# A graph layer on one core: column offsets 32 to a load, and other shares for ScalarE and VectorE

## The chip, the cores and the metric

The kernel runs on one core of a Trainium2 chip. The metric is device time in microseconds (us) of one execution. A core has five engines that run side by side, each with its own instruction stream in order: TensorE (PE; its weight loads are listed as PEld), VectorE (DVE), ScalarE (ACT), GpSimd (POOL) and SyncE (SP, which only issues DMAs here). An engine's sequencer reads instructions, loads registers and puts work in the engine's queue. It can be ahead of the engine.

## The reference

200,000 edges, sorted by destination, join 12,500 nodes of 128 features. Each node averages the normalised features of its sources, adds its own, and goes through three dense layers:

```python
h = jnp.maximum(_layernorm(x, axis=-1), 0.0)          # x: (12500, 128)
msgs = h[src]                                         # src, dst: (200000,), dst sorted
agg = jax.ops.segment_sum(msgs, dst, num_segments=n)
agg = agg / jnp.maximum(deg, 1.0)[:, None]
h = jax.nn.relu(agg @ Wg + h @ Ws + bg)
h = jnp.tanh(h @ W1 + b1)                             # 128 -> 512
h = jnp.tanh(h @ W2 + b2)                             # 512 -> 512
return x + (h @ W3 + b3)                              # 512 -> 128
```

## The kernel before, in words

**Chunks.** The edges are cut into 1563 chunks of 128. For a chunk PE multiplies the 128 source rows with a one-hot matrix (`oh`, 128 edges by a window of 24 nodes), so that the sum lands in an accumulator of a block of 512 nodes (`agg`) or of the edge between two blocks (`edge`). VectorE makes the one-hots of eight chunks at a time, a group (line 540, `onehot`), two groups ahead in the program, in five buffers used in turn: a group waits until PE has used the one that stood in its buffer.

**Three ways to the rows.** 80 "raw" chunks, ten groups spread over the run, are gathered from the raw input at the start and normalised on VectorE. Most others are gathered from the normalised table in HBM by GpSimd, with one indirect DMA for each chunk (line 451, `gather`), up to 26 chunks ahead of PE (`AHEAD`, the buffers of `rows_in`). The remaining chunks are built without a gather. `tab` holds the table turned, features on partitions and nodes along the row, in the core's memory. A chunk's rows turned are 128 of its columns, picked by offsets that stand in registers:

- ScalarE's lane (`column_copies`, `cols1`): one ACTIVATE makes two columns (line 518; 64 for a chunk).
- VectorE's lane (`column_pairs`, `cols2`): one SCALAR_TENSOR_TENSOR makes two columns (line 500).

PE then turns the chunk (line 444), ScalarE copies it out as `turned` (line 518), and PE uses it like gathered rows. VectorE corrects the one-hot of such a chunk (line 547), since the pairs hold a sum and one of two terms.

**Offsets.** `offsets` (line 461) loads `LOADS` offsets from `places` into registers with one TENSOR_LOAD; the instructions behind it name these registers:

```python
loads, vs = nc.values_load_multi_w_load_instructions(
    places[r : r + 1, q // EVERY, p0 : p0 + LOADS], engines=[kind], ...
```

PE loads its own registers in the same way, with the places of its windows (line 654: up to 16 values, fewer where a raw group lies in the row of 16 chunks).

**Order.** The program is written chunk by chunk, and each engine runs it in that order. `SHARES` says how many chunks go to ScalarE's and VectorE's lanes; they are spread evenly over every fourth chunk from number 80 up to 1480 (ScalarE) and 1540 (VectorE). `load_times` spreads the making of columns over the chunks before use: ScalarE's in steps of four columns, 28 chunks ahead, VectorE's in steps of `LOADS` columns, 36 ahead. The turn stands 14 chunks ahead. The dense layers of a finished block are put between the chunks in small pieces; from chunk 1312 on a planner does it by costs.

Of the kernel before, what the change touches and what calls it, by code (L numbers as in the profile page):

```python
# [45 lines left out]
BEHIND = 2  # L46
EVERY = 4
AT = 3
SHARES = 72, 72
FROM, ENDS = 80, (1480, 1540)  # L50
MARGIN = 28
SUMS_AT, BANK = 1 << 25, 2048
AHEAD_OF_USE = 2
EDGE_BANK = 7
TOGETHER = 4
LOADS = 16

# [21 lines left out]
def windowed(ctx, tc, x, src, dst, Wg, Ws, bg, W1, b1, W2, b2, W3, b3, out, flag):  # L81
# [50 lines left out]
    for c in slots:  # L132
        shares = [n / k * (c < end) for n, k, end in zip(SHARES, within, ENDS)]
        owed = [o + n for o, n in zip(owed, [*shares, 1 - sum(shares)])]
# [323 lines left out]
    def offsets(lane, c, p0):  # L458
        r, q = divmod(c, CPR)
        kind = (mybir.EngineType.Activation, mybir.EngineType.DVE)[lane]  # L460
        loads, vs = nc.values_load_multi_w_load_instructions(  # L461
            places[r : r + 1, q // EVERY, p0 : p0 + LOADS], engines=[kind], min_val=TAB_AT,
            max_val=TAB_AT + (N - 1) * 4,
            skip_runtime_bounds_check_because="src holds rows of x, as the indirect DMAs take it to",
        )
        for ld in loads:
            if lane and last:
                tc.add_manual_dep(
                    ld.ins, last[0].ins.name,
                    mybir.DependencyInfo(mybir.DependencyClass.NoSync, mybir.DependencyReason.DATA), reason="issue_after",  # L470
                )
            tc.keep_in_program_order(ld)
        vs = [v.with_bounds(min_val=TAB_AT, max_val=TAB_AT + (N - 1) * 4, guaranteed_mod_val=0, out_of_modulus=4) for v in vs]
        return enumerate(vs, p0)
# [3 lines left out]
    def two(lane, c, p0):  # L478

        by_pair = columns[c].rearrange("p (t i) -> p i t", t=2)  # L480
        at_v = dict(offsets(lane, c, p0))
        for p in range(p0, p0 + LOADS, 2):
            a, b = (tab[:, bass.ds((at_v[q] - TAB_AT) // 4, 1)] for q in (p, p + 1))
            yield p, by_pair[:, p // 2], a, b

    def column_copies():
        for c in lanes[0]:
            columns[c] = ed.tile([P, P], F32, name="cols1", bufs=4)
            for p0 in range(0, P, LOADS):
                for p, to, a, b in two(0, c, p0):  # L490
# [4 lines left out]
    def column_pairs():  # L495
        for c in lanes[1]:
            columns[c] = ed.tile([P, P], F32, name="cols2", bufs=6)
            for p0 in range(0, P, LOADS):
                for p, to, a, b in two(1, c, p0):
# [387 lines left out]
    def load_times(lane):  # L887
# [4 lines left out]
        use = [max(FROM - 46 + MARGIN, use[0] - step), *use]  # L892
        some = LOADS if lane else TOGETHER
        for i in range(len(lanes[lane])):
# [486 lines left out]
```

## Time and profile before

| | before |
|---|---|
| median of 3 runs | 1805.02 us (1799.81 to 1805.12) |
| profiled execution | 1800.16 us |
| its span, first to last instruction | 1798.4 us |
| PE busy | 1399.2 us, 78% |
| VectorE busy | 1034.4 us, 58% |
| ScalarE busy | 1534.3 us, 85% |
| GpSimd busy | 1348.5 us, 75% |
| granted TensorE clock, mean | 0.83 of full speed |

The times are medians of whole executions; the profile is one execution. Busy time counts an engine's own work only: loads of registers and waits are not in it, so an engine that is 58% busy can still have little time to spare. "Issue" in a profile's row is idle time in which the engine waited for no other engine that the profile shows; ahead of the columns it is the load of the offsets.

### The profile page before, as it was taken

The numbers are of one execution on the slowest core, as the hardware profiler recorded it, in microseconds if no ns is written. First come the engines' busy times: TensorE is split into PE (matmuls) and PEld (weight loads), VectorE is DVE, ScalarE is ACT, GpSimd is POOL, SyncE is SP. The second block draws the span as 40 slices with busy tenths as digits, with TensorE's granted clock in tenths as the row PEclk, the third lists the DMA queues.
The fourth block names the chain that finished last, engine by engine and source line by source line (L and its number), as shares of the span: only waits on it lengthen the run. The fifth ranks groups of instructions, "written<-read, shape, count | busy, mean of one in ns | idle before, by whom it ended". The sixth has DMA issues, their size and how long they took to land.

```text
span 1798.4 us, 26668 instructions
## 1 busy us (share of the span) xinstructions
PE 1399.2 (78%) x5410; PEld 926.5 (52%) x5410; DVE 1034.4 (58%) x5580; ACT 1534.3 (85%) x5169; POOL 1348.5 (75%) x1428
## 2 busy tenths in 40 slices
PE   0047576878787888897888888787888888779998
PEld 0036454555455555555555555545555554555567
DVE  7965866666655656566565665556556655435400
ACT  1213999999999999999999999999999999998223
POOL 7777777777777777777777777777777777777774
PEclk9999999767887786877867868879787788778998
DMA  8954222222222222222222222222222222222221
GB/s 209 242 140 139 55 67 58 64 61 70 58 73 71 59 73 71 57 73 71 71 59 71 71 59 71 71 59 73 71 59 71 71 56 73 71 65 71 59 62 45
DMA packets 129832, 138.77 MB, mean 77 GB/s; under 512 B 30119, under 2 KB 106019, under 8 KB 129464
## 3 DMA queue, kind: packets, MB, share of 16 engines
q0 software_dynamic: 45408, 93.09, 19.9%
q1 hardware_dynamic: 80974, 40.37, 8.3%
q10 hardware_dynamic: 3276, 3.51, 0.7%
q14 instruction: 128, 1.05, 0.2%
q8 instruction: 46, 0.75, 0.2%
HBM read 123.84 MB, written 13.03 MB: 76 GB/s over the span
## 4 chain that ended last, share of the span: by engine, by line
ACT 29%; PE 25%; DMA 19%; issue 13%; POOL 9%; ACTq 4%; DVE 0%; DVEq 0%; POOLq 0%
ACT cols L518 25%; DMA rows<-htab,scol 19%; PE pm L441 17%; PE agg L441 6%; POOL rows L451 4%; POOL raw L217 4%; ACTq L461 4%; ACT h L518 3%; PE edge L441 2%; PE pm L444 1%; ACT turned L518 0%; ACT rd L521 0%; ACT o L521 0%; DVE cols L500 0%; DMA raw<-in_x_dram,rsrc 0%
## 5 line engine op out<-in xcount | busy, mean ns | idle before, releaser
L451 POOL DMA_INDIRECT rows<-htab,scol x1339 | 1267.8, 947 | 408.0 <-issue 226.7
L518 ACT ACTIVATE cols<-both_first,tab 128x2 f32<-128x2 f32 x4608 | 1351.2, 470 | 3.8 <-issue 1.9
L441 PE MATMUL pm<-h,w 128*128 128x512 f32 (+4 forms) x1344 | 795.0, 692 | 25.0 <-ACT h L518 20.5
L500 DVE SCALAR_TENSOR_TENSOR cols<-first_only,tab 128x2 f32<-128x2 f32 x4608 | 666.6, 218 | 250.4 <-issue 249.3
L441 PEld LDWEIGHTS agg<-oh,rows 128*128 128x128 f32 x1928 | 394.6, 253 | 426.8 <-DMA rows<-htab,scol 260.5
L441 PE MATMUL agg<-oh,rows 128*128 128x24 f32 x1928 | 398.7, 307 | 177.2 <-DMA rows<-htab,scol 172.2
L540 DVE TENSOR_TENSOR oh<-shared,dloc 128x192 f32<-128x192 f32 x186 | 65.5, 354 | 356.6 <-PE agg L441 211.0
L441 PEld LDWEIGHTS pm<-h,w 128*128 128x128 f32 x1344 | 243.6, 229 | 33.5 <-ACT h L518 22.4
L441 PEld LDWEIGHTS edge<-oh,rows 128*128 128x128 f32 x750 | 144.0, 233 | 164.8 <-DMA rows<-htab,scol 89.4
L441 PE MATMUL edge<-oh,rows 128*128 128x24 f32 x750 | 145.9, 289 | 63.3 <-DMA rows<-htab,scol 59.4
L518 ACT ACTIVATE h<-pm,b2c 128x512 f32<-128x512 f32 (+4 forms) x112 | 76.9, 689 | 51.6 <-PE pm L441 51.6
L217 POOL DMA_INDIRECT raw<-in_x_dram,rsrc x80 | 79.8, 998 | 25.6 <-issue 23.8
L587 DVE TENSOR_SCALAR_CACHE_REDUCE nearby<-nearby,parity 128x656 uint8<-128x656 uint8 x98 | 86.8, 886 | 0.0
L518 ACT ACTIVATE h<-pm,b1c 128x512 f32<-128x512 f32 (+4 forms) x112 | 76.6, 694 | 11.8 <-PE pm L441 11.2
L521 ACT COPY tab<-pm 128x512 f32<-128x512 f32 (+1 forms) x25 | 14.4, 577 | 68.1 <-PE pm L444 68.1
L340 PE MATMUL pm<-ident,idx_f 98*128 98x98 f32 x32 | 5.7, 373 | 82.5 <-DVE idx_f L334 54.4
L441 PEld LDWEIGHTS agg<-oh,turned 128*128 128x128 f32 x196 | 45.1, 258 | 36.6 <-issue 33.0
L444 PE MATMUL pm<-ident,cols 128*128 128x128 f32 x144 | 49.2, 342 | 10.7 <-ACT h L518 5.4
L518 ACT ACTIVATE turned<-pm 128x128 f32<-128x128 f32 x144 | 50.3, 349 | 7.4 <-PE pm L444 7.4
L740 DVE TENSOR_TENSOR mT<-agg,sums 128x136 f32<-128x136 f32 (+6 forms) x57 | 15.3, 272 | 71.3 <-PE agg L441 61.9
L441 PE MATMUL pm<-ident,h 128*128 128x128 f32 (+1 forms) x196 | 43.8, 309 | 14.4 <-ACT h L518 14.3
L270 ACT ACTIVATE sq<-xt 128x1280 f32<-128x1280 f32 (+3 forms) x11 | 12.7, 1153 | 44.6 <-DVE xt L267 35.4
(129 smaller groups left out, 850.8 us busy)
## 6 DMA issues: line engine op xcount, KB each, us to landing
rows<-htab,scol POOLq DMA_INDIRECT x1339
nearby<-bytes_at SPq DMA_DIRECT2D x98, 82.0 KB
xb<-htab SPq DMA_DIRECT2D x24, 256.0 KB
xb<-in_x_dram SPq DMA_DIRECT2D x23, 256.0 KB
out_dram<-o SPq DMA_DIRECT2D x23, 256.0 KB
xt<-in_x_dram SPq DMA_DIRECT2D x8, 640.0 KB
htab<-h SPq DMA_DIRECT2D x8, 640.0 KB
raw<-in_x_dram,rsrc POOLq DMA_INDIRECT x80
```

The costliest lines, as they stand in the source:

```text
L217: nc.gpsimd.indirect_dma_start(out=t[:, j, :], out_offset=None, in_=x, in_offset=bass.IndirectOffsetOnAxis(ap=rsrc[:, g, j : j + 1], axis=0),)
L270: nc.scalar.activation(sq, xt, AF.Square)
L441: tc.keep_in_program_order(nc.tensor.matmul(*a, **k))
L444: tc.keep_in_program_order(nc.tensor.transpose(*a, **k))
L451: nc.gpsimd.indirect_dma_start(out=r, out_offset=None, in_=htab, in_offset=bass.IndirectOffsetOnAxis(ap=scol[:, c : c + 1], axis=0),)
L461: loads, vs = nc.values_load_multi_w_load_instructions(places[r : r + 1, q // EVERY, p0 : p0 + LOADS], engines=[kind], min_val=TAB_AT, max ...
L500: last[:] = [tc.keep_in_program_order(nc.vector.scalar_tensor_tensor(to, first_only, a, b.to_broadcast([P, 2]), op0=ALU.mult, op1=ALU.subtract
L518: tc.keep_in_program_order(nc.scalar.activation(*a, **k))
L521: tc.keep_in_program_order(nc.scalar.copy(*a))
L540: newest[:] = [nc.vector.tensor_tensor(oh[:, :k, :w], lane[:, None, :w].to_broadcast([P, k, w]), dloc[:, g * GRP : g * GRP + k][:, :, None ...
L587: done = nc.vector.tensor_scalar(w, w, parity[:, t % 2 : t % 2 + 1], None, op0=ALU.is_equal, op1=ALU.add, accum_out=found[:, t : t + 1])
L740: nc.vector.tensor_tensor(out, s, t, op=ALU.add)
```

## The change

```diff
-SHARES = 72, 72
+SHARES = 70, 98
-LOADS = 16
+LOADS = 32
```

The first line takes two chunks from ScalarE's lane and gives 26 more to VectorE's. So 168 chunks are built from columns in place of 144, and 1315 are gathered in place of 1339. The chunks of both lanes move to other places, since they are spread anew. The second line makes each load of offsets twice as long: four loads for a chunk in place of eight, each ahead of 16 instructions in place of 8, on both engines. VectorE's steps grow with it from 16 to 32 columns.

GpSimd's queue at the place where the raw gathers end and the others begin, and on to the end of the program (`raw` and `rows` are the buffers written):

```order
 L217 DMA raw_173<-in_x_dram,rsrc 128x128 x8
 L217 DMA raw_182<-in_x_dram,rsrc 128x128 x8
-L451 DMA rows<-htab,scol 128x128 x1339
+L451 DMA rows<-htab,scol 128x128 x1315
 L1346 TENSOR_LOAD flag
```

Nothing else moved there: 24 gathers fewer in one unbroken row.

VectorE's stream where its first columns stand, before (`raw_146` is the sixth raw group, `ohr` a scratch buffer, `oh_204` the first one-hot buffer, in its third use):

```order
L267 SCALAR_TENSOR_TENSOR raw_146<-shared,raw_146 128x1024
L272 TENSOR_TENSOR ohr<-raw_146 128x8x128
L273 TENSOR_REDUCE shared<-ohr 128x8
L540 TENSOR_TENSOR oh_204<-shared,dloc 128x192
L587 TENSOR_SCALAR nearby,found<-nearby,parity 128x656
L547 SCALAR_TENSOR_TENSOR oh_204<-shared,partner,oh_204 128x24
L461 TENSOR_LOAD places
L500 SCALAR_TENSOR_TENSOR cols_1370<-first_only,tab 128x2 x8
```

The same place in the changed kernel:

```order
L267 SCALAR_TENSOR_TENSOR raw_146<-shared,raw_146 128x1024
L461 TENSOR_LOAD places
L500 SCALAR_TENSOR_TENSOR cols_1323<-first_only,tab 128x2 x16
...
L500 SCALAR_TENSOR_TENSOR cols_1648<-first_only,tab 128x2 x16
L272 TENSOR_TENSOR ohr<-raw_146 128x8x128
L273 TENSOR_REDUCE shared<-ohr 128x8
L461 TENSOR_LOAD places
L500 SCALAR_TENSOR_TENSOR cols_1648<-first_only,tab 128x2 x16
L461 TENSOR_LOAD places
L500 SCALAR_TENSOR_TENSOR cols_1648<-first_only,tab 128x2 x16
L540 TENSOR_TENSOR oh_204<-shared,dloc 128x192
```

Seven loads and 112 pairs now stand ahead of the one-hots of that group; before they came behind it.

ScalarE's stream in the middle of the run, before (`cols_22034` is one chunk's columns, `h_512` a dense layer's output):

```order
L461 TENSOR_LOAD places
L518 ACTIVATE cols_22034<-both_first,tab 128x2 x8
L461 TENSOR_LOAD places
L518 ACTIVATE cols_22034<-both_first,tab 128x2 x6
L518 ACTIVATE turned<-pm 128x128
L518 ACTIVATE cols_22034<-both_first,tab 128x2 x2
L461 TENSOR_LOAD places
```

And in the changed kernel:

```order
L461 TENSOR_LOAD places
L518 ACTIVATE cols_27273<-both_first,tab 128x2 x16
L461 TENSOR_LOAD places
L518 ACTIVATE cols_27273<-both_first,tab 128x2 x4
L518 ACTIVATE h_512_27519<-pm,bgc 128x512
L518 ACTIVATE cols_27273<-both_first,tab 128x2 x12
L461 TENSOR_LOAD places
```

The loads stand half as densely; the other work lies between the columns as before.

## The prediction

> **What bounds the kernel now.** I read the page's groups first, to see which engine's work is serial, then the waits, then the windows. These are three groups of the page and the waits of POOL and, from 200 to 1600 us, of PE:
>
> ```profile
> L451 POOL DMA_INDIRECT rows<-htab,scol x1339 | 1267.8, 947 | 408.0 <-issue 226.7
> L518 ACT ACTIVATE cols<-both_first,tab 128x2 f32<-128x2 f32 x4608 | 1351.2, 470 | 3.8 <-issue 1.9
> L500 DVE SCALAR_TENSOR_TENSOR cols<-first_only,tab 128x2 f32<-128x2 f32 x4608 | 666.6, 218 | 250.4 <-issue 249.3
> ...
> POOL rows L451 <- issue: 226.7, 744, 0.3
> POOL rows L451 <- DMA rows<-htab,scol: 75.2, 247, 0.3
> POOL rows L451 <- PE agg L441: 57.6, 189, 0.3
> ...
> PE agg L441 <- DMA rows<-htab,scol: 142.4, 201, 2.2
> PE edge L441 <- DMA rows<-htab,scol: 47.8, 73, 1.6
> PE pm L441 <- ACT h L518: 20.4, 9, 5.6
> ```
>
> GpSimd issues one gather after another. Each costs (1267.8 + 408.0) / 1339 = 1.2515 us with the gap ahead of it, and no wait is longer than 0.3 us, whatever it is put down to: a fixed pace, never held up by a full buffer. In the body PE waits 190 us for gathered rows and 20 us for ScalarE. The last gather of the timeline starts 16.6 us before the end of the 1798.4 us span:
>
> ```profile
> 1781.76 0.94 POOL L451 DMA_INDIRECT rows<-htab,scol  x1 [0.30 <-issue]
> ```
>
> So GpSimd's pace sets the end, and a short tail follows it. ScalarE is nearly as full (3.8 us idle ahead of all its columns) but starts its last load of offsets at 1650.4 us (row below). What comes off the gathers comes off the end only as long as the other engines keep up.
>
> **Fewer gathers.** The change takes 168 chunks off GpSimd, not 144: 1315 gathers, not 1339. 24 x 1.2515 = **30.0 us less**, on the path. Raw gathers, tail and setup stay.
>
> **ScalarE.** A chunk of columns costs it 64 x 1351.2 / 4608 = 18.8 us. Two fewer: -37.5 us. Every chunk off GpSimd is also copied out once after PE turned it, 24 copies more; a group by shape, and two rows of the timeline:
>
> ```profile
> L518 ACT ACTIVATE turned<-pm 128x128 f32<-128x128 f32 x144 | 50.3, 349 | 7.4 <-PE pm L444 7.4
> ...
> 714.59 0.33 ACT L518 ACTIVATE turned<-pm 128x128 f32<-128x128 f32 x1
> 714.75 1.57 ACT L518 ACTIVATE cols<-both_first,tab 128x2 f32<-128x2 f32 x5
> ```
>
> By the mean that is +8.4 us, by the distance to the next start (0.16 us) +3.8. ScalarE saves 29 to 34 us where GpSimd saves 30, so it stays just as close behind. PE gains 24 turns of 0.34 us (8 us, beside its 190 us of waits for rows).
>
> **The longer load.** No trace shows a load of 32 values. The nearest rows are the loads of 16 on the two engines, and PE's loads of window places, which hold 16 values or, where a raw group opens the row, 8 (the loads at 418.9 and 412.3 us):
>
> ```profile
> L461 DVEq TENSOR_LOAD <-places x576: 1093/1123/1781, 172.5 to 1704.4; - x192
> L461 ACTq TENSOR_LOAD <-places x576: 1004/1043/1620, 172.6 to 1650.4; - x192
> ...
> L654 PEldq TENSOR_LOAD <-spots x1: 604/604/604, 412.3 to 412.3; - x1
> ...
> L654 PEldq TENSOR_LOAD <-spots x1: 1137/1137/1137, 418.9 to 418.9; - x1
> ```
>
> Eight more values cost 533 ns, so sixteen more cost 1.07 us: about 2.17 us on VectorE and 2.11 on ScalarE. From below, a load might stay at 1.1 us; from above I let it be 10% over the line, 2.4 us. I take the line: it goes through both of PE's points and 1.04 to 1.12 us of the other engines agree with it at 16. Halving the number of loads then saves next to nothing.
>
> The Trainium skill, "DMA: Bandwidth & Descriptors", section "Latency and other measured facts", gives a register load a floor of about 600 ns, to be spread over more work; with such a fixed part the 392 loads that VectorE is spared for 98 chunks would be worth 235 us of its time, and rival 1 below would be out. PE's load of 8 values at 604 ns is near that figure, but its 1137 at 16 leaves a fixed part of only 71 ns, and the rows decide.
>
> On ScalarE the load is hidden. The columns begin with an unbroken run; the fifth load of that stretch is at 179.7 us:
>
> ```profile
> 173.97 27.13 ACT L518 ACTIVATE cols<-both_first,tab 128x2 f32<-128x2 f32 x97 [1.03 <-DVE oh L547]
> ...
> L461 ACTq TENSOR_LOAD <-places x5: 1020/1027/1218, 172.6 to 179.7; - x5
> ```
>
> Its own first instruction is the 33rd of the run, at 173.97 + 32 x 0.28 = 182.9 us: 3.2 us, or 11 instructions, are queued when the load starts. A load of 2.1 us leaves 1.1 us to spare. Cost: nothing.
>
> On VectorE it isn't hidden, since eight pairs last only 1.1 us:
>
> ```profile
> 701.54 1.14 DVE L500 SCALAR_TENSOR_TENSOR cols<-first_only,tab 128x2 f32<-128x2 f32 x8 [0.97 <-issue]
> 702.99 1.14 DVE L500 SCALAR_TENSOR_TENSOR cols<-first_only,tab 128x2 f32<-128x2 f32 x8 [0.31 <-issue]
> 704.44 1.17 DVE L500 SCALAR_TENSOR_TENSOR cols<-first_only,tab 128x2 f32<-128x2 f32 x8 [0.30 <-issue]
> ```
>
> Sixteen columns take 1.45 us: 1.10 of load and 0.35 in which the sequencer passes on eight pairs. For 32 columns I reckon 2.17 + 0.70 = 2.87 us, while sixteen pairs keep the engine 1.14 + 8 x 0.131 = 2.19 us: 0.68 us idle for each load. That needs about ten pairs queued when the next load starts. VectorE can hold that many:
>
> ```profile
> 724.04 3.33 DVE L500 SCALAR_TENSOR_TENSOR cols<-first_only,tab 128x2 f32<-128x2 f32 x24
> ...
> L461 DVEq TENSOR_LOAD <-places x4: 1097/1107/1116, 719.3 to 724.7; - x4
> ```
>
> The last of these loads, at 724.7 us, belongs to the 17th pair, which starts at 726.1: eleven were ahead of it.
>
> **VectorE's budget from 200 to 1600 us.** All instructions, then the columns' alone (after the length stand the busy us of PE, PEld, DVE, ACT and, in the first, POOL), and VectorE's waits there:
>
> ```profile
> 200.00:1600.00 1400.00, 1153.34 (x4252) 740.23 (x4251) 833.07 (x4921) 1378.98 (x4744) 1058.75 (x1121) 0.80 0.25 66
> ...
> 200.00:1600.00 1400.00, 45.40 (x133) 29.46 (x133) 609.18 (x4215) 1275.95 (x4347) 0.80 0.25 66
> ...
> DVE cols L500 <- issue: 226.1, 486, 1.9
> DVE oh L540 <- PE agg L441: 169.0, 55, 6.9
> DVE oh L540 <- PE edge L441: 120.4, 38, 9.7
> ```
>
> Waits other than for loads are 1400 - 833.1 - 226.1 = 341 us, nearly all at the one-hot groups, whose buffers PE has not freed: VectorE runs ahead. The window holds 4215 / 4608 = 91.5% of the pairs. 26 more chunks there are 1522 pairs of 0.1445 us, +220 us, and 22 corrections of a one-hot (0.24 us), +5. Load waits go from 226 to 359 loads x 0.68 = 244, +18. Together +243 us, against 341 less the 27.5 us by which the window shrinks: **some 70 us to spare in 1370**. That is thin. The threshold is a cycle of 3.07 us for a load and its sixteen pairs; beyond it every 0.1 us costs 36 us. If each load exposed its whole extra 1.07 us over today's mean of 0.43 (226.1 us by 527 loads), +312 us more than today would be needed in load waits, and VectorE would be late by 220. I don't take that end: the long gaps, such as 0.97 us above, follow a wait for a one-hot buffer, so they occur where VectorE has time, and go when it is behind.
>
> Early on it is behind: VectorE starts its columns with seven loads (20 us) ahead of a one-hot group that today goes first. Up to 26 x 1.25 = 32 us of lateness stay in the row buffers before GpSimd feels them.
>
> **The sum.** 1800.16 us for the profiled execution, 1.8 more than its span; less 30.0 is 1770.1. The median shown is 4.9 us above that execution, so a median after may lie at 1770 to 1775. I say **1773**, with 1765 to 1780 for this case.
>
> **The rivals.**
> 1. *VectorE becomes the bound; slower.* Should a load of 32 cost over 2.4 us, or the queue hold fewer than ten pairs, the cycle passes 3.07 us. With eight queued, the load would start only after (16 - 8) x 0.131 = 1.05 us and the cycle be 1.05 + 2.17 + 0.09 = 3.3 us: short by about 85 us in the body, one-hots late, buffers used up, about 1855 us. At 3.2 it gives 1810 to 1820. Against it: PE's two loads and the eleven queued pairs. The Trainium skill, "Advanced Engine Details and Errata", section "Engine Queue Depths", gives 8 for both engines, which is this case; the two loads above disagree with 11. Chance 0.14, 0.03 of it for fewer queued pairs.
> 2. *ScalarE's columns come late; part of the gain.* Between 1540 and 1700 us PE waits for ScalarE's layers, not for rows:
>
> ```profile
> PE pm L441 <- ACT h L518: 24.9, 7, 5.6
> ```
>
> GpSimd was not held up, since the row buffers cover 32 us, but 8 us more would reach it. A tenth of a microsecond for each of 280 loads that isn't hidden is 28 us: 1780 to 1799. Together with early lateness of VectorE that isn't made up: 0.14.
> 3. *GpSimd's pace stretches when VectorE is busier; no change.* 1.7% would eat it all: 1795 to 1805. The groups of gathers at 200 to 300 us and at 1700 to 1790 us, where VectorE goes from 70% busy to almost idle:
>
> ```profile
> L451 POOL DMA_INDIRECT rows<-htab,scol x80 | 76.3, 954 | 24.4 <-issue 12.5 <-DMA rows<-htab,scol 5.2 <-PE agg L441 3.4
> ...
> L451 POOL DMA_INDIRECT rows<-htab,scol x67 | 63.2, 944 | 20.4 <-issue 7.3 <-DMA rows<-htab,scol 3.7 <-PE pm L441 3.7
> ```
>
> 10 ns of 1250 at most: 0.05. That the change doesn't do what it says is excluded by the order: 1315 gathers and sixteen pairs behind each load.
>
> **How the numbers follow.** Forecast 0.67, rivals 0.14, 0.14 and 0.05. The range from 1765 to 1800 holds the first, the second, and half of the third. Faster by over 0.3% (about what a measurement can tell from no change; below 1799.6): 0.67 + 0.14 = 0.81. Within 0.3%: 0.05. Slower: 0.14.
>
> **What would show it.** Right: 1315 gathers at 1.25 us with no wait over 0.3; loads of 32 at 2.1 to 2.2 us; cycles of 2.8 to 2.9 us on VectorE; its waits at one-hots down from 289 us to some 50; ScalarE without idle time at loads. Wrong: PE waiting for one-hots or turned columns by tens of microseconds, GpSimd waits of whole microseconds, a load above 2.4 us.

## The result, and the profile after

| | before | change |
|---|---|---|
| median, 5 runs each | 1802.51 us (1799.81 to 1805.12) | 1822.22 us (1816.43 to 1825.28) |
| ratio, 95% interval | | 1.0096 [1.0076, 1.0117] |
| profiled execution, its span | 1800.16, 1798.4 us | 1818.1, 1816.3 us |
| granted TensorE clock, mean | 0.83 | 0.81 |

The change is slower by 1.0%. The forecast of 1773 us was wrong in its sign, and the range up to 1800 missed it by 22 us. The ratios, here and below, compare undisturbed executions alone and are not the quotients of the medians beside them: two of the four runs of e4 and one of the four of f4 were slow ones. Four groups of the changed kernel's page (count, then busy us and mean ns of one, then idle us ahead of the group and what ended most of it):

```profile
L451 POOL DMA_INDIRECT rows<-htab,scol x1315 | 1245.4, 947 | 430.0 <-issue 220.3
L518 ACT ACTIVATE cols<-both_first,tab 128x2 f32<-128x2 f32 x4480 | 1310.5, 455 | 13.2 <-issue 13.1
L500 DVE SCALAR_TENSOR_TENSOR cols<-first_only,tab 128x2 f32<-128x2 f32 x6272 | 882.1, 217 | 424.5 <-issue 416.4
...
L540 DVE TENSOR_TENSOR oh<-shared,dloc 128x192 f32<-128x192 f32 x186 | 64.1, 345 | 32.2 <-PE agg L441 28.8
```

The 24 gathers are gone, yet all gathers with their gaps take 1245.4 + 430.0 = 1675.4 us, against 1267.8 + 408.0 = 1675.8 before. GpSimd's waits and the last gather of the timeline:

```profile
POOL rows L451 <- PE agg L441: 86.6, 214, 5.8
...
POOL rows L451 <- PE edge L441: 35.9, 92, 3.9
```

```profile
1781.49 0.94 POOL L451 DMA_INDIRECT rows<-htab,scol  x1 [0.30 <-PE pm L441]
```

A wait of 0.3 us is the pace itself; waits of up to 5.8 us are row buffers that PE had not freed. So the 30 us that came off the count were given back, one for one, as waits for buffers. The last gather starts at 1781.5 us, as before, but the span ends 34.8 us behind it, not 16.6. The sum is -0.4 + 18.2 = +17.8 us; the spans differ by 17.9. The next view is the waits from 200 to 1600 us:

```profile
DVE cols L500 <- issue: 373.0, 341, 2.8
...
PE pm L441 <- DVE mT L742: 83.8, 16, 16.1
...
PE pm L441 <- ACT h L518: 63.1, 27, 6.7
...
PE pm L444 <- ACT turned L518: 44.8, 21, 6.4
...
ACT h L518 <- PE pm L441: 39.7, 12, 6.6
...
PE agg L441 <- DMA rows<-htab,scol: 27.4, 43, 1.3
```

PE's wait for rows at `agg` fell from 142.4 us to 27.4; it waits for VectorE's transposed sums (`mT`), for ScalarE's layers and for turned columns. VectorE no longer waits for a one-hot buffer at all in this stretch (289 us before), which leaves it two things: work and loads. The window's row says how much (busy us of PE, PEld, DVE, ACT, POOL):

```profile
200.00:1600.00 1400.00, 1086.55 (x4219) 724.74 (x4240) 1006.31 (x6368) 1333.70 (x4593) 1042.40 (x1103) 0.77 0.25 65
```

VectorE's 1006.3 busy and 373.0 at loads make 1379 of 1400 us. **VectorE is full.** The chain that ended last says the same, before and then after:

```profile
ACT 29%; PE 25%; DMA 19%; issue 13%; POOL 9%; ACTq 4%; DVE 0%; DVEq 0%; POOLq 0%
```

```profile
DVE 38%; ACT 27%; issue 15%; PE 8%; POOL 5%; DVEq 3%; DMA 2%; ACTq 2%; POOLq 0%
```

The loads themselves cost what was reckoned, 2.15 us on VectorE and 2.01 on ScalarE (ns, least, median and most; then the first and last start):

```profile
L461 DVEq TENSOR_LOAD <-places x392: 2097/2154/3078, 162.9 to 1738.3; - x196
L461 ACTq TENSOR_LOAD <-places x280: 1945/2014/2656, 171.3 to 1661.8; - x140
```

So does the cycle of a load with its sixteen pairs, where pairs follow pairs. But VectorE's timeline also has another kind of gap:

```profile
705.94 2.31 DVE L500 SCALAR_TENSOR_TENSOR cols<-first_only,tab 128x2 f32<-128x2 f32 x16 [1.18 <-issue]
708.78 2.23 DVE L500 SCALAR_TENSOR_TENSOR cols<-first_only,tab 128x2 f32<-128x2 f32 x16 [0.53 <-issue]
...
717.32 0.38 DVE L547 SCALAR_TENSOR_TENSOR oh<-shared,partner,oh 128x24 f32<-128x24 f32 x2
719.72 2.19 DVE L500 SCALAR_TENSOR_TENSOR cols<-first_only,tab 128x2 f32<-128x2 f32 x16 [2.02 <-issue]
```

Back to back the cycle is 708.78 - 705.94 = 2.84 us (2.87 was reckoned). Behind line 547 the gap is 2.02 us, nearly the load's whole length. The load between those two rows:

```profile
L461 DVEq TENSOR_LOAD <-places x1: 2101/2101/2101, 717.2 to 717.2; - x1
```

It starts at 717.2 us, as the first of line 547's two instructions goes to the engine, and not earlier, while the pairs of 714.61 us still run. Line 547 corrects a one-hot that VectorE itself has just written (`oh` stands on both sides of its arrow), so it has to wait for its own engine's result; the load behind it doesn't begin before that wait is over, and by then little is queued that could cover it. The gaps ahead of a run of pairs, sorted by the instruction that stands just ahead of that run, for the four kinds that hold nearly all of the time (worked out from the starts in the traces; k1 and k3 are experiments below, with 98 chunks on VectorE as in the change, k3 with loads of 16):

| ahead of the pairs | before: times, mean us | change | k1 | k3 |
|---|---|---|---|---|
| another pair, line 500 | 349, 0.34 | 181, 0.67 | 180, 0.68 | 547, 0.35 |
| correction, line 547 | 124, 0.62 | 140, 1.45 | 142, 0 | 141, 0.50 |
| reciprocal, line 598 | 21, 1.00 | 23, 2.02 | 23, 1.14 | 23, 0.96 |
| `mT`, line 742 | 20, 0.90 | 17, 1.82 | 26, 0.38 | 17, 0.84 |

Gaps between pairs came out at 0.67 us, where 0.68 was predicted. The number of those behind a correction goes by the corrected groups: k3 makes 784 loads and the change 392, but 141 and 140 of them stand behind a correction. And each grew by nearly the whole 1.03 us by which a load of 32 is longer than one of 16, from 0.50 to 1.45, where the gap between pairs grew by 0.32. How much of a load shows depends on what stands between the one-hot and its correction. Where the correction follows directly it is 2.03 us (9 times in the change); where line 587 lies between and covers part of the load, 1.34 (61 times; 0.30 at the 61 such places of k3). From before to the change, 124 x 0.62 = 77 us became 140 x 1.45 = 203.

### The profile page after: what moved, and what is told of

Its sections match the earlier page's. It is cut to its first block, busy times and chain, and to the rows that moved or that the text cites. A ratio compares the mean times of both kernels' runs of the same rounds, so it can differ in the third digit from the quotient of the medians.

```text
span 1816.3 us, 27733 instructions
## 1 busy us (share of the span) xinstructions
PE 1333.0 (73%) x5413; PEld 909.1 (50%) x5434; DVE 1238.3 (68%) x7268; ACT 1502.2 (83%) x5065; POOL 1326.1 (73%) x1404
## 4 chain that ended last, share of the span: by engine, by line
DVE 38%; ACT 27%; issue 15%; PE 8%; POOL 5%; DVEq 3%; DMA 2%; ACTq 2%; POOLq 0%
DVE cols L500 30%; ACT cols L518 23%; PE pm L441 7%; POOL raw L217 4%; DVEq L461 3%; DVE nearby L587 3%; ACT h L518 3%; DMA rows<-htab,scol 2%; DVE oh L540 2%; ACTq L461 2%; PE agg L441 1%; POOL rows L451 1%; DVE oh L547 1%; DVE mT L742 1%; DVE ohr L540 0%
## 5 line engine op out<-in xcount | busy, mean ns | idle before, releaser
L451 POOL DMA_INDIRECT rows<-htab,scol x1315 | 1245.4, 947 | 430.0 <-issue 220.3
L518 ACT ACTIVATE cols<-both_first,tab 128x2 f32<-128x2 f32 x4480 | 1310.5, 455 | 13.2 <-issue 13.1
L500 DVE SCALAR_TENSOR_TENSOR cols<-first_only,tab 128x2 f32<-128x2 f32 x6272 | 882.1, 217 | 424.5 <-issue 416.4
L441 PE MATMUL pm<-h,w 128*128 128x512 f32 (+4 forms) x1344 | 780.1, 680 | 89.5 <-ACT h L518 66.8
L441 PE MATMUL agg<-oh,rows 128*128 128x24 f32 x1892 | 359.6, 297 | 58.6 <-DMA rows<-htab,scol 53.2
L441 PEld LDWEIGHTS edge<-oh,rows 128*128 128x128 f32 x738 | 130.3, 216 | 105.7 <-issue 73.9
L441 PE MATMUL edge<-oh,rows 128*128 128x24 f32 x738 | 122.8, 267 | 23.7 <-DMA rows<-htab,scol 19.0
L441 PE MATMUL pm<-mT,wg 128*128 128x512 f32 (+4 forms) x56 | 44.1, 882 | 95.2 <-DVE mT L742 95.2
L444 PE MATMUL pm<-ident,cols 128*128 128x128 f32 x168 | 61.0, 363 | 54.5 <-ACT turned L518 25.9
L444 PEld LDWEIGHTS pm<-ident,cols 128*128 128x128 f32 x168 | 41.3, 246 | 62.2 <-ACT turned L518 28.5
```

The lines of the kernel that those rows point to most:

```text
L441: tc.keep_in_program_order(nc.tensor.matmul(*a, **k))
L444: tc.keep_in_program_order(nc.tensor.transpose(*a, **k))
L451: nc.gpsimd.indirect_dma_start(out=r, out_offset=None, in_=htab, in_offset=bass.IndirectOffsetOnAxis(ap=scol[:, c : c + 1], axis=0),)
L500: last[:] = [tc.keep_in_program_order(nc.vector.scalar_tensor_tensor(to, first_only, a, b.to_broadcast([P, 2]), op0=ALU.mult, op1=ALU.subtract
L518: tc.keep_in_program_order(nc.scalar.activation(*a, **k))
```

## The experiments

The theories. **A**: the loads that stand exposed behind an instruction of VectorE's own fill VectorE up. **B**: 98 chunks are too many for VectorE, whatever their loads. **C**: ScalarE's longer loads cost it the time. Later two more, on what remains of the tail: **D**: ScalarE is late with its columns, and PE ends behind it. **E**, its rival: the tail doesn't hang on ScalarE's share.

Two edits recur. Loads of a length for each lane (ScalarE's, VectorE's):

```diff
-LOADS = 32
+LOADS = 32, 16
...
-            places[r : r + 1, q // EVERY, p0 : p0 + LOADS], engines=[kind], min_val=TAB_AT,
+            places[r : r + 1, q // EVERY, p0 : p0 + LOADS[lane]], engines=[kind], min_val=TAB_AT,
```

And "loads ahead": VectorE's next load stands right behind the pairs of the step before, and the one-hots (with their corrections) come behind that load:

```diff
+            if i + 1 < len(steps):
+                at_v = dict(offsets(1, *steps[i + 1]))
+                early[:] = [mark[0]]
+            yield
...
+        if early:
+            tc.add_manual_dep(
+                newest[0].ins, early[0].ins.name,
...
```

### The deciding four, on one ordinary chip

The kernel before took 1804.58 us there (13 runs). `k0_change` is the change, `k1_ahead` adds loads ahead, `k2_act16` has `LOADS = 16, 32`, `k3_dve16` has `LOADS = 32, 16`.

> The change, as the mark for the three kernels beside it on the same chip. Both theories: 1.01 over the kernel before where that takes about 1800 us, 1.02 to 1.03 where it takes about 2150.

> The change with VectorE's loads moved ahead of the one-hot groups, nothing else. Theory A (idle time of exposed loads on VectorE): below the change by 1 to 2% where the kernel before takes about 2150 us, by 2 to 3% where about 1800. Theory B (98 chunks of pairs, whatever the loads): within 0.5% of the change. Theory C (ScalarE's loads): within 0.5% of the change.

> The change with loads of 16 on ScalarE alone. Theories A and B: within 0.5% of the change. Theory C: below it by 1 to 2%.

> The change with loads of 16 on VectorE alone, ScalarE keeps 32. Theory A: below the change by 1.5 to 2.5% where the kernel before takes about 2150 us, 1770 to 1785 us where that takes about 1800. Theories B and C: within 0.5% of the change.

| | us | ratio to before, 95% |
|---|---|---|
| k0, the change | 1823.30 | 1.0100 [1.0083, 1.0116] |
| k1, loads ahead | 1804.35 | 0.9997 [0.9987, 1.0007] |
| k2, 16 on ScalarE | 1822.86 | 1.0101 [1.0084, 1.0118] |
| k3, 16 on VectorE | 1791.99 | 0.9929 [0.9912, 0.9945] |

**C falls**: k2 is k0, though its loads on ScalarE are half as long:

```profile
L461 ACTq TENSOR_LOAD <-places x560: 1004/1044/1614, 172.9 to 1663.1; - x187
L461 DVEq TENSOR_LOAD <-places x392: 2097/2153/2805, 164.2 to 1738.4; - x196
```

**B falls** as the cause of the loss: k1 and k3 make the same 98 chunks. **A stands**: k1 makes the same loads, pairs and one-hots, with the loads ahead, and wins 19 us; k3 shortens them and wins 31. Neither edit is pure, since the program's order moves with it. By the traces, in k1 24 of 196 one-hot groups stand up to 80 pairs later than in the change, and 41 of the 188 instructions that make `mT` (lines 740 and 742), for which PE waits, 16 to 208 pairs sooner; in k3 all but two of these stay within 16 pairs, but 42 one-hot groups stand up to 112 pairs sooner. What the two runs share is the shorter idle time at loads, so the cause doesn't hang on either shift alone; how much of the 19 and the 31 us is due to the shifts wasn't tried. k1's groups, PE's wait for `mT` from 200 to 1600 us (83.8 in the change), and a stretch of VectorE's timeline:

```profile
L451 POOL DMA_INDIRECT rows<-htab,scol x1315 | 1245.6, 947 | 417.5 <-issue 227.3
...
L506 DVE SCALAR_TENSOR_TENSOR cols<-first_only,tab 128x2 f32<-128x2 f32 x6272 | 882.3, 217 | 174.2 <-issue 158.3
...
L549 DVE TENSOR_TENSOR oh<-shared,dloc 128x192 f32<-128x192 f32 x186 | 66.2, 357 | 143.1 <-issue 61.1
```

```profile
PE pm L441 <- DVE mT L756: 44.3, 9, 12.8
```

```profile
701.94 0.38 DVE L561 SCALAR_TENSOR_TENSOR oh<-shared,partner,oh 128x24 f32<-128x24 f32 x2
702.24 2.22 DVE L506 SCALAR_TENSOR_TENSOR cols<-first_only,tab 128x2 f32<-128x2 f32 x16
...
706.46 0.18 DVE L612 RECIPROCAL degs<-degs 128x4 f32<-128x4 f32 x1
708.66 2.30 DVE L506 SCALAR_TENSOR_TENSOR cols<-first_only,tab 128x2 f32<-128x2 f32 x16 [2.03 <-issue]
```

The lines are numbered anew (506 is 500, 561 is 547, 612 is 598, 756 is 742). Behind the correction the pairs now start at once, in all 142 cases. Idle time for loads is 158.3 + 61.1 = 219 us, not 416; some of it has moved ahead of the one-hots. The reciprocal, which reads what the instruction ahead of it wrote (`degs`), still has the load behind it here and in 13 of its 23 cases, and the gap is still 2.03 us: the same mechanism, left in place.

But neither k1 nor k3 reached the forecast of 1773, and the sizes that A expected are both missed: k1 lies 1.0% below the change, not 2 to 3%, and k3 above 1770 to 1785. So idle time at loads isn't all that holds the end. k3's gathers, PE's waits from 200 to 1600 us, the last gather, and the chain:

```profile
L451 POOL DMA_INDIRECT rows<-htab,scol x1315 | 1246.5, 948 | 400.8 <-issue 229.5
...
PE pm L441 <- ACT h L518: 58.1, 28, 5.0
...
PE pm L441 <- ACT turned L518: 47.3, 24, 4.2
PE pm L444 <- ACT turned L518: 45.9, 19, 6.8
```

```profile
1752.41 0.94 POOL L451 DMA_INDIRECT rows<-htab,scol  x1 [0.30 <-PE pm L441]
```

```profile
ACT 58%; DVE 13%; PE 11%; issue 6%; DMA 5%; ACTq 4%; POOL 1%; DVEq 1%; SPq 0%; POOLq 0%
```

Now GpSimd does save its time: 1246.5 + 400.8 = 1647.3 us, 28.5 less than before, and its last gather starts 29.4 us sooner. But the span ends 34.8 us behind that gather, and the chain is ScalarE's. The end of ScalarE's last column (from the traces) lies at 1670 us in the change, 1657 in k1, 1641 in k3, and the span ends 146 us later each time (1816.3 - 1670 in the change). The last gather's is as constant, 34.8 to 34.9 us, but in k3 PE comes to the last rows some 20 us after their gathers' starts (3 to 5 in most of the body before), so it isn't gathers that it waits for. That made D.

### Fewer chunks for ScalarE

The kernel before took 1803.55 us on this chip (7 runs). `m1_66_98` is k3 with other shares; `m2_ahead_66_98` is m1 with loads ahead; `m3_ahead_64_104` is m2 with two chunks less on ScalarE and six more on VectorE.

```diff
-SHARES = 70, 98
+SHARES = 66, 98
```

> k3 (loads of 16 on VectorE, 32 on ScalarE) with four chunks fewer for ScalarE: shares 66 and 98, 1319 gathers. k3 left 18 us of the 30 unfound: GpSimd's row of gathers was 28 us shorter, but the tail behind it 18 us longer. Theory D (ScalarE, never idle but for waits, is late with its columns and layers; its last columns end at 1641 us in k3 and the kernel 146 us later): its columns end about 60 us earlier, the tail shrinks to 17 to 22 us and the time is 1775 to 1782 us where the kernel before takes about 1804. Theory E (PE itself needs the longer tail, for its layers are all behind): tail 30 us or more and 1788 to 1796 us.

> m1 with VectorE's loads ahead of the one-hot groups as well. Theory D: within 3 us of m1, since VectorE holds nobody up any more. If VectorE's lateness still counts: 3 to 10 us below m1. Theory E: 1785 to 1796 us.

> m2 with shares 64 and 104: 1315 gathers as in the change, two chunks fewer for ScalarE and six more for VectorE. Theory D with room left on VectorE: 5 us below m2 (four gathers), 1768 to 1776 us. If VectorE is full at 98 chunks: above m2 by 5 to 20 us.

| | us | ratio to before, 95% |
|---|---|---|
| m1 | 1779.51 | 0.9866 [0.9849, 0.9882] |
| m2 | 1776.85 | 0.9848 [0.9831, 0.9864] |
| m3 | 1775.57 | 0.9842 [0.9826, 0.9858] |

m1 gathers four chunks more than k3 and is 12.5 us faster, comparing medians on two chips. Its gathers, PE's waits in the body, the last gather and the chain:

```profile
L451 POOL DMA_INDIRECT rows<-htab,scol x1319 | 1250.8, 948 | 402.0 <-issue 256.6
...
PE agg L441 <- DMA rows<-htab,scol: 146.7, 216, 2.0
...
PE pm L441 <- ACT h L518: 8.7, 6, 2.1
```

```profile
1758.86 0.94 POOL L451 DMA_INDIRECT rows<-htab,scol  x1 [0.30 <-issue]
```

```profile
PE 25%; issue 18%; ACT 18%; DVE 16%; DMA 13%; POOL 8%; DVEq 2%; ACTq 1%; POOLq 0%
```

PE waits for rows again, ScalarE's share of the chain falls from 58% to 18%, and the tail is 1778.3 - 1758.86 = 19.5 us. **D stands and E falls.** One part of the expectation missed: ScalarE's columns end only 18 us sooner (1623, not 1641), since ScalarE then waits for PE; that end lies 155 us ahead of the span's, so it is no longer what sets it. m2 lies 2.7 us below m1. The intervals overlap, but all four runs of m2 (1774.48 to 1777.95 us) lie below all four of m1 (1778.46 to 1780.57), so a small gain is likely: once VectorE has room, moving its loads is worth about 0.2%. m3 lies 1.3 us below m2, and their runs overlap; D expected 5. Its tail grows to 24.5 us, which takes back part of the four gathers. So 66 and 98 with 16 offsets on VectorE is a version that beats the kernel before by 1.3%; the two refinements add some 0.2%.

### The earlier runs, on chips where everything was slower

The runs before those fell on three chips on which the kernel before itself took 2141 to 2166 us. These numbers stand beside that kernel on the same chip, and beside nothing else. `e1`, `f1`, `g1` and `h1` are the change with `LOADS = 16`; `e2` is the kernel before with `LOADS = 32`; `e3` and `f3` have loads ahead; `e4` and `f4` are k2; `f5` is `LOADS = 16` and loads ahead; `g0` is the change.

> The change with loads of 16 again, shares 70 and 98 kept. Theory A (VectorE is the bound, because a load of 32 that stands behind an instruction which waits for VectorE's own result starts with an empty queue and is idle time nearly whole, 1.5 to 2.0 us against 0.6 to 1.0 for a load of 16): load waits on VectorE fall from 424 to about 325 us and the time to 1770 to 1785 us. Theory B (98 chunks of pairs are more than VectorE can make beside its other work, whatever the loads): stays at 1810 or more. Theory C (ScalarE's longer loads delay the dense layers and the turned columns, on which PE waits): 1770 to 1790, with ScalarE's idle time at loads gone and VectorE's load waits no shorter.

> Shares 72 and 72 as before, loads of 32. Theory A: VectorE's load waits rise from 250 to about 315 us, but 341 us stand free in the body, so 1798 to 1806 us, no change from before. Theory B: the same. Theory C: 1812 us or more, since ScalarE's loads are those of the change.

> The change, with each of VectorE's loads moved ahead of the one-hot group that stands between it and its pairs, right behind the pairs of the load before. Pairs, loads and shares are unchanged. Theory A: nearly every load now starts with about ten pairs queued and idles 0.65 to 0.7 us, load waits fall from 424 to about 270 us, time 1770 to 1785 us. Theory B: load waits fall but the time stays at 1810 or more. Theory C: unchanged at 1815 to 1825 us.

> The change with loads of 16 on ScalarE alone; VectorE keeps loads of 32. Theory A and theory B: as the change, 1814 to 1826 us. Theory C: 1770 to 1795 us.

> Loads of 16 with shares 70 and 98, again, since on the first chip the kernel before took 19% longer than in its other runs and GpSimd's gathers had waits of whole microseconds that theory and change don't explain. Where the kernel before takes about 1800 us: theory A (exposed loads make VectorE the bound) 1770 to 1785 us, load waits about 325 us; theory B (98 chunks of pairs are too many for VectorE, whatever the loads) 1810 or more; theory C (ScalarE's longer loads) 1770 to 1790 with VectorE's load waits no shorter than in the change.

> The change with each of VectorE's loads ahead of the one-hot group. Where the kernel before takes about 1800 us: theory A 1770 to 1785 us and load waits of about 270 us; theory B 1810 or more with short load waits; theory C 1815 to 1825.

> Loads of 16 on ScalarE, of 32 on VectorE. Where the kernel before takes about 1800 us: theories A and B as the change, 1814 to 1826 us; theory C 1770 to 1795.

> Loads of 16 and each ahead of the one-hot group, shares 70 and 98: both remedies. Theory A: load waits about 250 us, the least of all, and GpSimd's pace the bound again, 1768 to 1780 us where the kernel before takes about 1800. Theory B: 1810 or more. Theory C: as with loads of 16 alone.

> The change itself, unaltered, beside the kernel before. Its ratio is 1.010 where the kernel before takes about 1800 us. On chips where it takes 2140 to 2170 us (there every engine shows extra stalls of 1 to 2 us) theories A and B expect the same ratio as with loads of 16 on ScalarE alone, 1.010 to 1.017; theory C expects more than that kernel's.

> Loads of 16 with shares 70 and 98, beside the change on the same chip. Theory A: below the change by 2 to 3% where the kernel before takes about 1800 us (1770 to 1785 us), by 0.5 to 1.5% where it takes about 2150. Theory B: within 0.5% of the change on either. Theory C: as theory A in time, but VectorE's load waits as in the change.

> One look at loads of 16 with shares 70 and 98, in search of a chip on which the kernel before takes about 1800 us. There theory A expects 1770 to 1785 us and load waits of about 325 us on VectorE, theory B 1810 or more. Where the kernel before takes about 2150, both expect within 1% of it.

| | us | before there | ratio, 95% |
|---|---|---|---|
| e1, 70/98, 16 on both | 2141.81 | 2140.96 | 1.0007 [0.9978, 1.0035] |
| e2, 72/72, 32 on both | 2142.61 | 2140.96 | 1.0003 [0.9973, 1.0033] |
| e3, loads ahead | 2156.73 | 2140.96 | 1.0075 [1.0042, 1.0109] |
| e4, 16 on ScalarE | 2193.94 | 2140.96 | 1.0168 [1.0068, 1.0267] |
| f1, as e1 | 2182.74 | 2166.03 | 1.0068 [1.0039, 1.0096] |
| f3, as e3 | 2179.22 | 2166.03 | 1.0071 [1.0045, 1.0097] |
| f4, as e4 | 2196.10 | 2166.03 | 1.0106 [1.0039, 1.0173] |
| f5, 16 on both, loads ahead | 2170.56 | 2166.03 | 1.0023 [0.9984, 1.0062] |
| g0, the change | 2188.21 | 2140.97 | 1.0259 [1.0189, 1.0329] |
| g1, as e1 | 2145.83 | 2140.97 | 1.0029 [1.0000, 1.0058] |
| h1, as e1, one run each | 2142.63 | 2142.09 | |

Times that were expected around 1800 us are misses here, since these chips are slower for every kernel. e1's gathers and two of GpSimd's waits:

```profile
L451 POOL DMA_INDIRECT rows<-htab,scol x1315 | 1248.8, 950 | 743.8 <-issue 304.0
...
POOL rows L451 <- PE agg L441: 193.0, 141, 17.3
POOL rows L451 <- remote: 124.4, 92, 5.1
```

A gather itself takes the 950 ns of any other run, but the gaps are 743.8 us in place of the change's 430.0, with single waits of 17 us. GpSimd is held up here, and its own pace isn't the bound, so fewer gathers need not shorten anything; e1, with its 24 fewer, is level with before. No trace of the kernel before on such a chip was kept.

Long loads with 72 chunks on VectorE cost nothing (e2), and with 98 they cost 2.6% (g0). The other ratios lie between, in no clean order: on the first and third chips 16 on both engines is level or nearly so (e1, g1), but on the second it is 0.7% behind, as loads ahead are (f1, f3); both remedies together are level (f5). Shorter loads on ScalarE alone leave 1.1 to 1.7% (e4, f4). That is less than g0's 2.6%, on other chips, and g0 was expected at 1.010 to 1.017 by A and B, and above the kernel with 16 on ScalarE by C. So these chips leave A against C open; k2 against k0, on one chip, decides it. Three chips give 1.0007, 1.0068 and 1.0029 for one kernel, and the first two intervals don't meet, so small differences between chips say nothing.

## Why the prediction was wrong

**Fewer gathers: right, but not kept.** The count fell by 24 and the pace is no rival (k3: 1647.3 / 1315 = 1.2527 us each, before 1.2515). Of the 30 us, 28.5 are there in k3's row of gathers and 30.5 in m3's (1244.5 + 400.8 = 1645.3).

**The price of a load: right.** 2.154 us against 2.17 and 2.014 against 2.11; sixteen more values cost 1.03 us on VectorE (1.07 was reckoned). The floor of 600 ns that the Trainium skill gives ("DMA: Bandwidth & Descriptors", "Latency and other measured facts") is again no fixed part of a load here: twice the values took 1.92 times as long.

**The back-to-back cycle: right.** 2.84 us against 2.87, mean gap 0.67 against 0.68. Of the 392 loads, 206 begin with eleven instructions of VectorE still to start, and none with more (from the starts in the trace). By the 8 queued instructions that the Trainium skill gives ("Advanced Engine Details and Errata", "Engine Queue Depths") the cycle was estimated at 3.3 us; the trace disagrees with it again.

**VectorE's budget: this step failed.** The prediction put every one of 359 loads in the body at 0.68 us, and set the longer gaps aside in one sentence: "the long gaps, such as 0.97 us above, follow a wait for a one-hot buffer, so they occur where VectorE has time, and go when it is behind". They don't go. They follow instructions that wait for VectorE's own result, the corrections above all, whether VectorE is early or late, and each grew by nearly all that was added to the load. The mean gap over all 392 loads is 416.4 / 392 = 1.06 us, so the mean cycle is 2.19 + 1.06 = 3.25 us, past the 3.07 that the prediction gave as its threshold. By its own sum 359 x (1.06 - 0.68) = 136 us more: where 70 us were to spare, 66 were short. In the change's body the load waits came to 373.0 us, not 244. Another term was too high: the pairs were put at 0.1445 us each, though sixteen take 2.19 / 16 = 0.137 by the prediction's own row. In the change 5648 pairs took 794.7 us from 200 to 1600 us, 0.141 each, which makes its 5737 pairs 22 us cheaper and the shortage, as an estimate, some 44 us. The two rows ahead of that 0.97 us gap, in VectorE's timeline of before, had told it:

```profile
699.94 0.35 DVE L540 TENSOR_TENSOR oh<-shared,dloc 128x192 f32<-128x192 f32 x1
700.33 0.24 DVE L547 SCALAR_TENSOR_TENSOR oh<-shared,partner,oh 128x24 f32<-128x24 f32 x1
```

This one-hot had not waited for a buffer (no idle time is noted ahead of it), and the gap came all the same.

**Rival 1 is what happened**, with neither of its triggers: the load stayed at 2.15 us, and runs of pairs show no shorter queue. At a cycle of 3.2 us it gave 1810 to 1820; measured is 3.25 and 1822. That the two agree so closely is in part luck, since the pairs were priced too high and the early and ScalarE's lateness below were not in that sum. The mechanism was priced; its way in was missed.

**"The early lateness stays in the row buffers": half right.** From the starts of gathers and of the matmuls that use them, PE runs 3 to 5 us behind the gathers through most of the run before. In the change this jumps to 15 us by gather 150 (means of 50 gathers), soon after the place where VectorE's columns now stand ahead of the one-hots, and is never made up; it is 28 us by gather 700 and 33 at its most, with single ones at 40. The buffers hold 26 x 1.25 = 32 us, and from there on GpSimd waits. In m1 the lag is 6 us at the same early place, 3 to 6 after it, and 7 at its most, near the end.

**"ScalarE stays just as close behind": the second failed step.** Its columns did get shorter by 40.7 us (1351.2 to 1310.5; 37.5 were reckoned), but they ended at 1670 us, where before it was 1657. ScalarE lost the time waiting, first here (the Sqrt of a raw group's statistics):

```profile
290.87 0.30 ACT L276 ACTIVATE shared<-shared,eps 128x80 f32<-128x80 f32 x1 [14.26 <-DVE oh L547]
```

and then for PE (39.7 us at `h` in the body, 16.0 before by the same view). An engine that is full can't make up such a wait; k3 shows what it costs once VectorE is cured (1792), and m1 that it was ScalarE (1780). Rival 2 had a late ScalarE, but by loads that aren't hidden; these cost little (13.1 us idle ahead of all its columns, 1.9 before), and k2, with loads half as long, gains nothing.

**The clock.** It is 0.81 in the change and 0.83 before, and doesn't explain the loss: the four runs of k0 took 1821.1 to 1824.2 us at 0.81 to 0.84, the fastest of them at 0.82 and the slowest at 0.84. PE's largest group of matmuls even got shorter, 680 ns each against 692 (first the page of before, then of the change).

```profile
L441 PE MATMUL pm<-h,w 128*128 128x512 f32 (+4 forms) x1344 | 795.0, 692 | 25.0 <-ACT h L518 20.5
```

```profile
L441 PE MATMUL pm<-h,w 128*128 128x512 f32 (+4 forms) x1344 | 780.1, 680 | 89.5 <-ACT h L518 66.8
```

**What stays open.** k1 idles 219 us for loads on VectorE and k3 298, and yet k3 is 12 us faster. Their steps differ as well (32 columns or 16), so that one-hots wait for longer runs in k1, ScalarE's columns end 16 us later, and other work stands elsewhere in the order, as said above; which of these it is wasn't tried. Nor were 66 and 98 with the long loads, nor with 16 on both engines.

## What to carry to other kernels

Sort idle gaps by the instruction that stands ahead of them before giving all of them one price: a register load behind an instruction that waits for its own engine's result is exposed for up to its full length (here 1.45 us of 2.15 on average behind a correction), and making loads longer and fewer makes exactly those gaps longer without making them fewer. Put such a load ahead of that instruction (19 us in k1, where other work moved too), or keep it short (31 us in k3). And when work is moved from the bound to two engines that are both nearly full, check each one's time at each stage: after the first was cured here, the second held the end, and the gain came only with less work for it.

## What the runs showed of the hardware

- A register load costs by its length almost alone: 604 ns for 8 values and 1137 for 16 on PE, 1123 for 16 and 2154 for 32 on VectorE, some 65 ns for each value more.
- A register load that stands behind an instruction waiting for its own engine starts only when that one is handed on (717.2 us above, with the pairs ahead of it running from 714.61), and its engine idles for up to the whole load (2.02 of 2.10 us there).
- On the three slower chips the kernel before took 2141 to 2166 us, in place of 1803 to 1805, with the same instructions. In e1 a gather itself took the 950 ns of any other run, but its gaps grew, 124.4 us of them put down to "remote" (0.3 us in the change's trace). The granted clock of the kernel before was 0.76 to 0.79 there and 0.81 to 0.84 on the two ordinary chips, but PE's largest group of matmuls took 719 ns in e1, 4% over the 692 of before, where the whole took 19% longer. What causes it is open.
